# Two rows of results from four mixtures of rows, in two of three bands of two 3x3 convolutions

## The chip, the cores and the metric

The kernel runs on one core of a Trainium2 chip. Time is the device time in microseconds (us); lower is better. The core has a matrix engine (TensorE, PE in the profile, with its weight loads as PEld), two engines for elementwise work (VectorE, DVE; ScalarE, ACT), a general one (GpSimd, POOL) and a sequencer that issues transfers (SyncE, SP). TensorE writes its results to a small accumulator memory (PSUM)[...]; everything else works in SBUF, the on-chip memory.

## What is computed

The input x has the shape (4, 128, 64, 64): four images, 128 channels, 64 rows of 64. First comes an attention layer, then a block of two convolutions. Cut to what matters here:

```python
def conv_block(x, w1, alpha1, gamma1, beta1, w2, alpha2, gamma2, beta2):
    out = conv3x3(x, lsq_quantize(w1, alpha1))      # sum over 9 shifted views, pad 1
    out = relu(batchnorm(out, gamma1, beta1))       # mean and variance over all images and positions
    out = conv3x3(out, lsq_quantize(w2, alpha2))
    out = batchnorm(out, gamma2, beta2)
    return relu(out + x)

# layer 0: group norm, q, k, v, softmax(q k) v with 4 heads, projection, plus x
x = attention_block(x, ...)
x = conv_block(x, ...)
```

The quantised weights are whole numbers from -4 to 3 times alpha; the kernel keeps the whole numbers and moves alpha into the batch norm.

## The kernel before

Channels lie on the 128 partitions throughout. The attention takes the first 2230 us or so and isn't changed. It leaves its result y in DRAM (`y0[b]`), from which the convolutions load it.

**Bands.** Each image is cut into four bands of 16 rows (`BR = 16`), 16 bands in all (`bandlist`), numbered m = 0 to 15. A band tile holds 18 rows of 66 values: the 16 rows, one more above and below, and a zero column on each side (`border`, memsets on POOL). For accuracy, each band is split in two (`split`, L573 and L574): `hi` is the band copied into the type float32r (a CAST on VectorE), `lo` is the band minus `hi` (a TENSOR_TENSOR on VectorE). The band tile, `hi` and `lo` come from one pool of nine buffers (`kpool`).

**One convolution** (`layer`). A band gives 1024 results per channel, in two halves of 512, each in a PSUM bank. A half is 18 matmuls of 128x128 weights by 512 values: nine taps for `hi`, nine for `lo` (`conv`, L782), so a band has 36. The accumulators of a band are one two-bank tile of the pool `pss` (three tiles); the last band uses the two single banks of `psa`. For each band the program issues first the matmuls, then `prepare(m)`, which gets band m+2 ready, and then for each half the batch-norm statistics on VectorE (L848) and the copy of the accumulator to `cv[b]` on ScalarE (L849). Each engine works off its own instructions in this order; they wait for each other through semaphores, and the order is that written in the program.

**What prepare does.** In the first convolution (`first`) it issues on SP the load of band m+3 and splits band m+2. In band 2 it also loads the second layer's weights into `raw_w`, in band 6 it casts them into `wq[1]`, and in band 5 it runs `count_bad`, a check of the attention's sums with one tiny matmul. In the second convolution (`second`) it makes band m+2 from the first layer's results: `relu_rows` applies batch norm and relu with one ScalarE ACTIVATE (L891), then casts `hi` (L894) and subtracts for `lo` (L895), both on VectorE; band 0 is made specially in two pieces (L913, L916). It also loads y again for the residual (`load_res`).

**Between and after.** The first convolution's batch norm needs all its results, so TensorE runs only a few idle matmuls between the two. After the second, each piece of the result is scaled, added to y (L948), rectified (L949) and stored.

Of the kernel before, what the change touches and what calls it, by code (L numbers as in the profile page):

```python
# [16 lines left out]
F32 = mybir.dt.float32  # L17
AF = mybir.ActivationFunctionType
ALU = mybir.AluOpType
# [3 lines left out]
P = 128  # L23
# [3 lines left out]
TAPS = 9  # L27
FB = 512
# [6 lines left out]
F32R = mybir.dt.float32r  # L35
# [43 lines left out]
def _fast_body(ctx, tc, x, norm_w, norm_b, qkv_wt, qkv_b, proj_wt, proj_b,  # L79
               w1, alpha1, gamma1, beta1, w2, alpha2, gamma2, beta2, out, cnt):  # L80
    nc = tc.nc
    B, C, H, W = x.shape
# [3 lines left out]
    NB = N // FB  # L86
# [3 lines left out]
    PW = W + 2  # L90
# [48 lines left out]
    wq = [const.tile([P, TAPS, P], F32R, name="wq0")]  # L139
    wqd = dram.tile([P, TAPS, P], F32, name="wqd")  # L140
# [414 lines left out]
    def band_tile(name):  # L555
        return stack_tile(name).rearrange("p (r w) -> p r w", w=PW)

    def border(t, g):

        nc.gpsimd.memset(f32(t)[:, :, 0:1], 0.0)  # L560
        nc.gpsimd.memset(f32(t)[:, :, W + 1 : W + 2], 0.0)
        r0, r1 = g * BR - 1, g * BR + BR + 1
        if r0 < 0:
            nc.gpsimd.memset(f32(t)[:, 0, 1 : 1 + W], 0.0)
        if r1 > H:
            nc.gpsimd.memset(f32(t)[:, BR + 1, 1 : 1 + W], 0.0)
        lo, hi = max(r0, 0), min(r1, H)
        return f32(t)[:, lo - r0 : hi - r0, 1 : 1 + W], lo, hi

    def split(t, name):  # L570

        hi, lo = band_tile(f"hi{name}"), band_tile(f"lo{name}")
        nc.vector.tensor_copy(hi, f32(t))  # L573
        nc.vector.tensor_tensor(lo, f32(t), f32(hi), ALU.subtract)  # L574
        return hi, lo

    raw, ready = {}, {}

    def load_band(b, g):
        raw[b, g] = t = band_tile(f"t0_{b}_{g}")  # L580
        inner, lo, hi = border(t, g)
        nc.sync.dma_start(out=inner, in_=y0[b].rearrange("p (h w) -> p h w", w=W)[:, lo:hi, :])

    def split_band(b, g):
        ready[0, b, g] = split(raw[b, g], f"0_{b}_{g}")


    halves = [ppool.tile([P, HEADS, FB], F32, name=f"xh{i}", tag="p") for i in range(2)]
# [6 lines left out]
    st = small.tile([P, NB, 6], F32, name="st0", tag="st")  # L595
# [144 lines left out]
    todo, parts = [], {}  # L740
# [29 lines left out]

    bandlist = [(b, g) for b in range(B) for g in range(H // BR)]

    def conv(parts, ps, j, w):
        hi, lo = parts
        r0 = j * RB
        n = 0
        for part in (hi, lo):
            for tap in range(TAPS):  # L780
                kh, kw = divmod(tap, 3)
                nc.tensor.matmul(ps.rearrange("p (r w) -> p r w", w=W), w[:, tap, :],  # L782
                                 part[:, r0 + kh : r0 + kh + RB, kw : kw + W],
                                 start=(n == 0), stop=(n == 2 * TAPS - 1))
                n += 1

    def conv_tile(i, b, g):
        return pss.tile([P, 2, FB], F32, name=f"c{i}_{b}_{g}", tag="s")
# [16 lines left out]

    mid = ctx.enter_context(tc.tile_pool(name="mid", bufs=1))
    cv = [mid.tile([P, N], F32, name=f"cv{b}") for b in range(B)]
    raw_w = mid.tile([P, TAPS, P], F32, name="raw_w")
    wq.append(mid.tile([P, TAPS, P], F32R, name="wq1"))


    a_q, a_g, a_n = ([small.tile([P, 1], F32, name=f"{n}{i}") for i in range(2)]
# [21 lines left out]
    def layer(i, prepare, done):  # L834


        st = mid.tile([P, B * NB, 6], F32, name=f"st{i}")
        end = mid.tile([P, 15], F32, name=f"end{i}")
        nc.gpsimd.memset(end[:, 0:1], float((B * NB - 2) * FB))
        for m, (b, g) in enumerate(bandlist[:-1]):  # L840
            ps = done[m] if m < len(done) else conv_tile(i, b, g)
            for j in range(2):
                if m >= len(done):
                    conv(ready[i, b, g], ps[:, j, :], j, wq[i])
            prepare(m)
            for j in range(2):
                c = 2 * g + j
                nc.vector.bn_stats(st[:, b * NB + c, :], ps[:, j, :])  # L848
                nc.scalar.copy(cv[b][:, c * FB : (c + 1) * FB], ps[:, j, :])  # L849
        nc.vector.bn_aggr(end[:, 1:3], st.rearrange("p j s -> p (j s)")[:, : 6 * B * NB - 12])  # L850
        nc.vector.tensor_scalar(end[:, 2:3], end[:, 2:3], float((B * NB - 2) * FB), None, ALU.mult)
        b, g = bandlist[-1]
        for j in range(2):
            ps = psa.tile([P, FB], F32, name=f"c{i}_last{j}", tag="a")
            conv(ready[i, b, g], ps, j, wq[i])
            c = 2 * g + j
            nc.vector.bn_stats(end[:, 3 + 6 * j : 9 + 6 * j], ps)
            nc.scalar.copy(cv[b][:, c * FB : (c + 1) * FB], ps)
        prepare(len(bandlist) - 1)
        keep_warm(10)  # L860
        return batch_norm(i, end)
# [11 lines left out]
    def first(m):  # L873
        if m == 5:
            count_bad()
        if m == 2:
            nc.sync.dma_start(out=raw_w, in_=wqd)
        if m == 6:
            nc.vector.tensor_copy(wq[1], raw_w)
        if 0 < m < len(bandlist) - 3:  # L880
            load_band(*bandlist[m + 3])
        if m + 2 < len(bandlist) and m > 0:
            split_band(*bandlist[m + 2])

    a1, c1 = layer(0, first, early)

    def relu_rows(b, g, t, r0, r1):

        inner, lo, hi = t["inner"]
        a, e = max(r0 + g * BR - 1, lo), min(r1 + g * BR - 1, hi)  # L890
        nc.scalar.activation(inner[:, a - lo : e - lo, :],  # L891
                             cv[b].rearrange("p (h w) -> p h w", w=W)[:, a:e, :], AF.Relu,
                             bias=c1, scale=a1)
        nc.vector.tensor_copy(t["hi"][:, r0:r1, :], f32(t["t"])[:, r0:r1, :])  # L894
        nc.vector.tensor_tensor(t["lo"][:, r0:r1, :], f32(t["t"])[:, r0:r1, :],  # L895
                                f32(t["hi"])[:, r0:r1, :], ALU.subtract)

    def relu_band(b, g, pieces=((0, BR + 2),)):
        t = {n: band_tile(f"{n}1_{b}_{g}") for n in ("t", "hi", "lo")}
        t["inner"] = border(t["t"], g)  # L900
        for r0, r1 in pieces:
            relu_rows(b, g, t, r0, r1)
        ready[1, b, g] = t["hi"], t["lo"]


    b0, g0 = bandlist[0]
    t = {n: band_tile(f"{n}1_{b0}_{g0}") for n in ("t", "hi", "lo")}
    t["inner"] = border(t["t"], g0)
    hi_inner, lo_row, hi_row = border(t["hi"], g0)
    for r0, r1 in ((0, RB + 2), (RB + 2, BR + 2)):  # L910
        a, e = max(r0 + g0 * BR - 1, lo_row), min(r1 + g0 * BR - 1, hi_row)
        for dst in (hi_inner.bitcast(F32R), t["inner"][0]):
            nc.scalar.activation(dst[:, a - lo_row : e - lo_row, :],  # L913
                                 cv[b0].rearrange("p (h w) -> p h w", w=W)[:, a:e, :], AF.Relu,
                                 bias=c1, scale=a1)
# [26 lines left out]
    for b in range(B):  # L942
        for j in range(4):
            for p in range(2 if b == j == 0 else 1):
                n = HN // 2 if b == j == 0 else HN
                y = res[b, j][:, p * n : (p + 1) * n]
# [464 lines left out]
```

## Time and profile before

| what | us |
|---|---|
| median of three runs | 2547.48 (2546.02 to 2547.59) |
| the profiled execution, its own time | 2548.74 |
| the span of its profile | 2547.0 |
| first convolution's band 0 starts (TensorE) | 2233.99 |
| first convolution's last matmuls end, the idle ones start | 2375.12 |
| second convolution: first relu, first matmul | 2377.87, 2378.84 |
| second convolution's last matmul, end | 2516.46 |
| then batch norm, residual, relu and stores, to the end | 30.5 |

The matmul times are read from the trace in order of time; the last row is 2547.0 - 2516.46. In the 20 us from 2410 to 2430, in the middle of the second convolution, TensorE is busy all the time, VectorE for 8.25 us, ScalarE for 4.80 and POOL for 0.66, at the full granted clock. A busy TensorE means that matmuls follow each other without a pause, and the ends of matmuls are modelled. In the rows of the profile, a group is a line, an engine, an operation, output<-inputs with their sizes, the count, then busy time in us, the mean in ns, and the engine's idle time just before with what ended it.

### The profile page before, as it was taken

The page shows a single profiled execution, that of the slowest core. Times are in us where ns is not written, and L with a number is a line of the kernel's source. Part 1 is how long each engine was busy: PE and PEld are TensorE (multiplying, and loading weights), DVE is VectorE, ACT ScalarE, POOL GpSimd, SP SyncE. Part 2 cuts the span into 40 slices and gives each one's busy share as a digit, 9 for nine tenths or more (in the row PEclk, how much of TensorE's full clock was granted, in tenths as well). Part 3 has the DMA queues.
Part 4 walks back from the last instruction along what each step waited for, and adds up shares of the span by engine and source line. Part 5 has one row for each costly group of instructions (what it writes and reads, how often), then busy time and mean ns, then how long its engine had stood idle before and what let it go on. Part 6 is the DMA issues. An engine that isn't in the chain of part 4 may idle for free.

```text
span 2547.0 us, 65043 instructions
## 1 busy us (share of the span) xinstructions
PE 2509.0 (99%) x28708; PEld 1503.6 (59%) x28708; DVE 2137.2 (84%) x1402; ACT 2087.4 (82%) x2278; POOL 281.6 (11%) x461
## 2 busy tenths in 40 slices
PE   9999999999999999999999999999999999999995
PEld 6555555555555555555555555555555555577774
DVE  6899888889988889889988888889999999954445
ACT  5999888999988999999988899989999999911224
POOL 2111111111011111110111111111000011000000
PEclk9999999999999999999999999999999999999998
DMA  6877667788757667797766666796666666745004
GB/s 193 192 185 169 168 173 181 171 203 182 184 132 190 170 152 169 164 231 164 173 163 172 157 166 158 191 203 150 149 138 144 146 145 149 150 90 160 1 1 166
DMA packets 148954, 403.86 MB, mean 159 GB/s; under 512 B 59416, under 2 KB 60184, under 8 KB 120120
## 3 DMA queue, kind: packets, MB, share of 16 engines
q0 software_dynamic: 45840, 280.39, 48.2%
q1 hardware_dynamic: 100952, 113.60, 16.9%
q10 hardware_dynamic: 1872, 5.64, 0.6%
q8 instruction: 227, 3.72, 0.6%
q14 instruction: 63, 0.52, 0.1%
HBM read 107.48 MB, written 56.42 MB: 64 GB/s over the span
## 4 chain that ended last, share of the span: by engine, by line
PE 92%; issue 3%; DMA 2%; DVE 1%; ACT 1%; ACTq 0%; POOL 0%; SPq 0%; POOLq 0%; DVEq 0%
PE s L442 41%; PE acc L456 36%; PE c L782 9%; DMA rm<-p 2%; PE l L488 1%; PE pq L317 1%; PE pk L317 1%; PE po L317 1%; PE pv L317 1%; DVE r L471 1%; ACT p L444 0%; ACT res L949 0%; DMA xh<-in_x_dram 0%; PE c_last L782 0%; DVE res L948 0%
## 5 line engine op out<-in xcount | busy, mean ns | idle before, releaser
L444 ACT ACTIVATE p<-s 128x1024 f32<-128x1024 f32 x2048 | 1950.5, 1032 | 201.6 <-PE s L442 154.5
L471 DVE TENSOR_TENSOR r<-r,p 128x2048 f32<-128x2048 f32 x768 | 1758.2, 2289 | 65.0 <-ACT p L444 14.5
L442 PE MATMUL s<-q,k 64*128 64x512 f32 x8192 | 1138.6, 409 | 1.7 <-ACT p L444 0.9
L456 PE MATMUL acc<-p,v 128*32 128x256 f32 x16384 | 1026.4, 383 | 0.0
L442 PEld LDWEIGHTS s<-q,k 64*128 64x128 f32 x8192 | 715.4, 184 | 410.3 <-issue 165.3
L456 PEld LDWEIGHTS acc<-p,v 128*32 128x32 f32 x16384 | 462.4, 109 | 483.7 <-issue 248.5
L466 POOL DMA_DIRECT2D rm<-p x160 | 139.5, 872 | 800.4 <-ACT p L444 535.5
L849 ACT COPY cv<-c 128x512 f32<-128x512 f32 x60 | 35.2, 586 | 200.1 <-DVE st L848 200.1
L782 PE MATMUL c<-hi,wq 128*128 128x512 f32 x540 | 139.1, 401 | 1.3 <-issue 1.3
L782 PE MATMUL c<-lo,wq 128*128 128x512 f32 x540 | 138.5, 400 | 0.0
L848 DVE BATCH_NORM_STATS2 st<-c 128x6 f32<-128x512 f32 x60 | 41.9, 699 | 103.9 <-PE c L782 83.4
L782 PEld LDWEIGHTS c<-hi,wq 128*128 128x128 f32 x540 | 101.2, 188 | 30.3 <-issue 2.1
L782 PEld LDWEIGHTS c<-lo,wq 128*128 128x128 f32 x540 | 101.6, 188 | 27.2
L352 DVE SCALAR_TENSOR_TENSOR kst<-pk,b,kst 128x512 fp32r<-128x512 f32 x32 | 24.0, 751 | 83.6 <-PE s L442 68.5
L469 DVE TENSOR_TENSOR r<-p,p 128x2048 f32<-128x2048 f32 x32 | 73.2, 2288 | 12.1 <-ACT p L444 11.1
L352 DVE SCALAR_TENSOR_TENSOR qst<-pq,b,qst 128x512 fp32r<-128x512 f32 x32 | 24.0, 751 | 58.2 <-PE s L442 47.3
L356 POOL DMA_DIRECT2D qd<-qst x31 | 23.6, 760 | 262.7 <-DVE qst L352 220.8
L492 POOL DMA_DIRECT2D r<-rm x31 | 26.2, 844 | 220.4 <-DMA rm<-p 95.1
L356 POOL DMA_DIRECT2D kd<-kst x27 | 20.0, 740 | 175.8 <-DVE kst L352 167.2
L488 PE MATMUL l<-r,ones 128*32 128x256 f32 (+1 forms) x504 | 37.7, 382 | 0.0
L464 POOL DMA_DIRECT2D rm<-p x32 | 17.8, 557 | 176.8 <-ACT p L444 93.4
L351 ACT ACTIVATE kst<-pk,b 128x512 fp32r<-128x512 f32 x32 | 22.3, 699 | 18.2 <-PE pk L317 18.2
(149 smaller groups left out, 739.3 us busy)
## 6 DMA issues: line engine op xcount, KB each, us to landing
rm<-p POOLq DMA_DIRECT2D x192, 1024.0 KB, 7.9
q<-qd SPq DMA_DIRECT2D x248, 128.0 KB
r<-rm POOLq DMA_DIRECT2D x31, 1024.0 KB, 7.6
x<-in_x_dram SPq DMA_DIRECT2D x86, 256.0 KB
k<-kd SPq DMA_DIRECT2D x124, 128.0 KB
qd<-qst POOLq DMA_DIRECT2D x31, 512.0 KB, 5.3
kd<-kst POOLq DMA_DIRECT2D x27, 512.0 KB, 4.8
y<-x POOLq DMA_DIRECT2D x32, 256.0 KB, 6.2
```

The costliest lines, as they stand in the source:

```text
L317: nc.tensor.matmul(out[cs, :], w[:, cs], x, start=True, stop=True)
L352: nc.vector.scalar_tensor_tensor(lo, ps[what], bias, t[:, 0, :], ALU.add, ALU.subtract)
L356: (nc.sync if start else nc.gpsimd).dma_start(out=dst[b, j].rearrange("s p n -> p s n"), in_=t)
L442: nc.tensor.matmul(s[:, i, :], k[r, half, c0 : c0 + P], q[r, half, part, :], start=(part == 0), stop=(part == 1))
L444: nc.scalar.activation(pts[step][:, 2 * half : 2 * half + 2, :], s, AF.Exp, scale=SCALE)
L456: nc.tensor.matmul(acc[n][h * D : (h + 1) * D, cs], v[:, kt % KB, h * D : (h + 1) * D], pt[:, h, cs], start=(kt == 0 and half == 0), stop= ...
L466: nc.gpsimd.dma_start(out=msum[n], in_=pt, accum_op=ALU.add)
L469: nc.vector.tensor_tensor(rsum[n], pts[step - 1], pt, ALU.add)
L471: nc.vector.tensor_tensor(rsum[n], rsum[n], pt, ALU.add)
L488: nc.tensor.matmul(t["l"][h * D : (h + 1) * D, cs], ones, r[:, h, cs], start=first, stop=end)
L782: nc.tensor.matmul(ps.rearrange("p (r w) -> p r w", w=W), w[:, tap, :], part[:, r0 + kh : r0 + kh + RB, kw : kw + W], start=(n == 0), stop ...
L848: nc.vector.bn_stats(st[:, b * NB + c, :], ps[:, j, :])
```

## The change

In 8 bands of the first convolution (m = 3, 4, 6, 7, 9, 10, 12, 13) and 9 of the second (2, 3, 5, 6, 8, 9, 11, 12, 14), two neighbouring rows of results are computed together. Let d0 to d3 be the four input rows that two rows of results y0 and y1 need, and g0, g1, g2 the weights of the three rows of taps (each with its three columns). Then four mixtures of rows are made, d0 - d2, d1 + d2, d2 - d1 and d1 - d3, each is multiplied by its weights, g0, (g0+g2+g1)/2, (g0+g2-g1)/2 and g2, and with the four products c0, a0, a1, c1

y0 = c0 + a0 + a1,  y1 = a0 - a1 - c1.

Each product is a sum of three columns of taps, for an upper and a lower part: 6 matmuls of 8 rows x 64 = 512 values, and four products make 24 matmuls for the 16 rows of a band.

- `mixed` takes the place of `split` in these bands: `outer` holds the first and last mixtures in turn (one VectorE instruction on 1056 values), `inner` the two in the middle (two on 528). The upper parts are copies on ScalarE, the lower parts subtractions on VectorE. Of a mixed band's seven tiles four come from `kpool` (the band itself among them), three come from a new pool `upper` of six.
- `conv_by_two` issues the matmuls, the a products first. They need four banks: one `pss` tile for a, and for c in turn a second `pss` tile or the two `psa` banks.
- `rows_of_two` combines them in `cv[b]`: one ScalarE copy and four VectorE instructions of 512 values, in rows two apart. The statistics are then taken from `cv`, in SBUF, where they were taken from PSUM.
- `mix_weights` makes the two mixed sets of weights, four VectorE instructions for each convolution.
- In bands that stay plain, the upper part is a ScalarE copy, except in the first three bands of the first convolution and band 0 of the second.
- The second layer's weights lie in a `kpool` buffer in place of their own, and are loaded in band 5 instead of 2.

```diff
-    def split(t, name):
+    def split(t, name, beside=True):
         hi, lo = band_tile(f"hi{name}"), band_tile(f"lo{name}")
-        nc.vector.tensor_copy(hi, f32(t))
+        if beside:
+            nc.vector.tensor_copy(hi, f32(t))
+        else:
+            nc.scalar.copy(hi, f32(t))
         nc.vector.tensor_tensor(lo, f32(t), f32(hi), ALU.subtract)
         return hi, lo
...
+    BY_TWO = (set((3, 4, 6, 7, 9, 10, 12, 13)), set((2, 3, 5, 6, 8, 9, 11, 12, 14)))
+
+    def mixed(t, name):
+        t = f32(t)
+        outer, inner = (stack_tile(f"{n}{name}")[:, : BR * PW].rearrange("p (r w) -> p r w", w=PW)
+                        for n in ("vo", "vi"))
+        nc.vector.tensor_tensor(f32(outer), t[:, 0:BR, :], t[:, 2 : BR + 2, :], ALU.subtract)
+        odd, even = t[:, 1 : BR + 1 : 2, :], t[:, 2 : BR + 2 : 2, :]
+        nc.vector.tensor_tensor(f32(inner)[:, : BR // 2, :], odd, even, ALU.add)
+        nc.vector.tensor_tensor(f32(inner)[:, BR // 2 :, :], even, odd, ALU.subtract)
+        def part(n):
+            if n == "uo":
+                return stack_tile(f"{n}{name}")[:, : BR * PW].rearrange("p (r w) -> p r w", w=PW)
+            return upper.tile([P, BR, PW], F32R, name=f"{n}{name}", tag="u")
+        hi, lo = ([part(n + k) for k in "oi"] for n in "ul")
+        for u, v in zip(hi, (outer, inner)):
+            nc.scalar.copy(u, f32(v))
+        for u, v, w in zip(hi, (outer, inner), lo):
+            nc.vector.tensor_tensor(w, f32(v), f32(u), ALU.subtract)
+        return [(o[:, 0::2, :], i[:, : BR // 2, :], i[:, BR // 2 :, :], o[:, 1::2, :])
+                for o, i in (hi, lo)]
...
     def split_band(b, g):
-        ready[0, b, g] = split(raw[b, g], f"0_{b}_{g}")
+        m = bandlist.index((b, g))
+        way = mixed if m in BY_TWO[0] else lambda t, name: split(t, name, m < 3)
+        ready[0, b, g] = way(raw[b, g], f"0_{b}_{g}")
...
-    raw_w = mid.tile([P, TAPS, P], F32, name="raw_w")
     wq.append(mid.tile([P, TAPS, P], F32R, name="wq1"))
+    upper = ctx.enter_context(tc.tile_pool(name="upper", bufs=6))
+    wmix = mid.tile([P, 2, 3, P], F32R, name="wmix")
+
+    def mix_weights(i):
+        g0, g1, g2 = (f32(wq[i])[:, 3 * k : 3 * k + 3, :] for k in range(3))
+        h = f32(stack_tile(f"wsum{i}"))[:, : 3 * P].rearrange("p (t o) -> p t o", o=P)
+        nc.vector.tensor_tensor(h, g0, g2, ALU.add)
+        nc.vector.tensor_scalar(h, h, 0.5, None, ALU.mult)
+        for k, f in enumerate((0.5, -0.5)):
+            nc.vector.scalar_tensor_tensor(wmix[:, k, :, :], g1, f, h, ALU.mult, ALU.add)
+
+    def conv_by_two(parts, a, c, i):
+        for m, ps, w in ((1, a[0], wmix[:, 0, :, :]), (2, a[1], wmix[:, 1, :, :]),
+                         (0, c[0], wq[i][:, 0:3, :]), (3, c[1], wq[i][:, 6:9, :])):
+            n = 0
+            for part in parts:
+                for kw in range(3):
+                    nc.tensor.matmul(ps.rearrange("p (r w) -> p r w", w=W), w[:, kw, :],
+                                     part[m][:, :, kw : kw + W], start=(n == 0), stop=(n == 5))
+                    n += 1
+
+    def rows_of_two(a, c, y):
+        even, odd = (y.rearrange("p (r e w) -> p r e w", e=2, w=W)[:, :, e, :] for e in range(2))
+        a0, a1, c0, c1 = (u.rearrange("p (r w) -> p r w", w=W) for u in (*a, *c))
+        nc.scalar.copy(odd, a1)
+        nc.vector.tensor_tensor(even, odd, a0, ALU.add)
+        nc.vector.tensor_tensor(odd, a0, odd, ALU.subtract)
+        nc.vector.tensor_tensor(even, even, c0, ALU.add)
+        nc.vector.tensor_tensor(odd, odd, c1, ALU.subtract)
+
+    mix_weights(0)
...
         for m, (b, g) in enumerate(bandlist[:-1]):
+            if m in BY_TWO[i]:
+                a = conv_tile(i, b, g)
+                a = [a[:, j, :] for j in range(2)]
+                if sorted(BY_TWO[i]).index(m) % 2:
+                    c = [psa.tile([P, FB], F32, name=f"c{i}_{b}_{g}{j}", tag="a") for j in "xy"]
+                else:
+                    c = pss.tile([P, 2, FB], F32, name=f"c{i}_{b}_{g}z", tag="s")
+                    c = [c[:, j, :] for j in range(2)]
+                conv_by_two(ready[i, b, g], a, c, i)
+                prepare(m)
+                y = cv[b][:, 2 * g * FB : (2 * g + 2) * FB]
+                rows_of_two(a, c, y)
+                for j in range(2):
+                    nc.vector.bn_stats(st[:, b * NB + 2 * g + j, :], y[:, j * FB : (j + 1) * FB])
+                continue
...
-        if m == 2:
-            nc.sync.dma_start(out=raw_w, in_=wqd)
+        if m == 5:
+            raw["w"] = f32(stack_tile("raw_w"))[:, : TAPS * P].rearrange("p (t o) -> p t o", o=P)
+            nc.sync.dma_start(out=raw["w"], in_=wqd)
         if m == 6:
-            nc.vector.tensor_copy(wq[1], raw_w)
+            nc.vector.tensor_copy(wq[1], raw["w"])
+        if m == 14:
+            mix_weights(1)
...
-        nc.vector.tensor_copy(t["hi"][:, r0:r1, :], f32(t["t"])[:, r0:r1, :])
+        nc.scalar.copy(t["hi"][:, r0:r1, :], f32(t["t"])[:, r0:r1, :])
...
     def relu_band(b, g, pieces=((0, BR + 2),)):
+        if bandlist.index((b, g)) in BY_TWO[1]:
+            t = band_tile(f"t1_{b}_{g}")
+            inner, lo, hi = border(t, g)
+            nc.scalar.activation(inner, cv[b].rearrange("p (h w) -> p h w", w=W)[:, lo:hi, :],
+                                 AF.Relu, bias=c1, scale=a1)
+            ready[1, b, g] = mixed(t, f"1_{b}_{g}")
+            return
```

More of the change, by code (lines that the diff above doesn't have):

```diff
@@ L577, in _fast_body @@
     raw, ready = {}, {}
+    bandlist = [(b, g) for b in range(B) for g in range(H // BR)]
+    BY_TWO = (set((3, 4, 6, 7, 9, 10, 12, 13)), set((2, 3, 5, 6, 8, 9, 11, 12, 14)))
[18 more added lines that the diff above has]
+                for o, i in (hi, lo)]
     def load_band(b, g):
@@ L769, in _fast_body @@
         run_weights(3)
-    bandlist = [(b, g) for b in range(B) for g in range(H // BR)]
     def conv(parts, ps, j, w):
```

## The prediction

> **What bounds the kernel now.** I read the busy totals first, then the chain of work that ended last over the convolutions, then the same stretch in slices of 20 us, then the groups of VectorE and ScalarE by shape, and last the order of time inside one band. TensorE is busy nearly all the time:
>
> ```profile
> PE 2509.0 (99%) x28708; PEld 1503.6 (59%) x28708; DVE 2137.2 (84%) x1402; ACT 2087.4 (82%) x2278; POOL 281.6 (11%) x461
> ```
>
> The attention is not touched, so only the last 310 us matter. In the chain, the second convolution is one unbroken run of matmuls:
>
> ```profile
> 2378.84 129.02 PE c L782 x540
> 2507.86 8.60 PE c_last L782 x36
> ```
>
> 129.02 / 540 = 0.2389 us a matmul, so a band of 36 takes 8.60 us. The slices (columns: stretch, its length, busy time of PE, PEld, DVE, ACT, POOL, granted clock, DMA) show who has room:
>
> ```profile
> 2410.00:2430.00 20.00, 20.00 (x86) 15.78 (x85) 8.25 (x9) 4.80 (x6) 0.66 (x8) 1.00 0.00 1
> ```
>
> VectorE is free for 11.75 us of 20, ScalarE for 15. Prices, from the groups:
>
> ```profile
> L895 DVE TENSOR_TENSOR lo<-t,hi 128x1188 fp32r<-128x1188 f32 x15 | 20.9, 1397 | 0.5
> L371 DVE TENSOR_TENSOR v<-pv,bvn 128x512 f32<-128x512 f32 x8 | 5.5, 683 | 0.0
> L688 DVE BATCH_NORM_STATS2 st<-x 128x6 f32<-128x512 f32 x24 | 16.2, 685 | 0.0
> L916 DVE TENSOR_TENSOR lo<-t,hi 128x528 fp32r<-128x528 f32 x1 | 0.7, 707 | 0.5 <-ACT t L913 0.5
> L849 ACT COPY cv<-c 128x512 f32<-128x512 f32 x60 | 35.2, 586 | 200.1 <-DVE st L848 200.1
> L891 ACT ACTIVATE t<-cv,bc,ba 128x1152 f32<-128x1152 f32 x8 | 10.7, 1353 | 0.0
> ```
>
> Last, how a plain band hands over from VectorE to ScalarE and back (order of time, second convolution):
>
> ```profile
> 2413.45 0.70 DVE L848 BATCH_NORM_STATS2 st<-c 128x6 f32<-128x512 f32 x1 [2.36 <-PE c L782]
> 2414.19 0.59 ACT L849 COPY cv<-c 128x512 f32<-128x512 f32 x1 [5.40 <-DVE st L848]
> 2414.81 0.70 DVE L848 BATCH_NORM_STATS2 st<-c 128x6 f32<-128x512 f32 x1 [0.65 <-ACT cv L849]
> 2415.54 0.58 ACT L849 COPY cv<-c 128x512 f32<-128x512 f32 x1 [0.76 <-DVE st L848]
> 2416.02 1.36 ACT L891 ACTIVATE t<-cv,bc,ba 128x1152 f32<-128x1152 f32 x1
> 2417.48 0.78 DVE L894 CAST hi<-t 128x1188 fp32r<-128x1188 f32 x1 [1.97 <-ACT t L891]
> 2418.29 1.40 DVE L895 TENSOR_TENSOR lo<-t,hi 128x1188 fp32r<-128x1188 f32 x1
> ```
>
> Statistics and copies alternate, then ScalarE makes the relu of the band two ahead, and VectorE stands still 1.97 us for it. Today this is free: TensorE has the next band ready. Starts also show that independent instructions overlap by about 0.09 us (2418.29 to the next start is 1.31 for a duration of 1.40), while one that needs the previous result starts about 0.03 after its end.
>
> [...] Here the clock column was still 1.00 up to 2523.00 and 0.55 in the next microsecond, with the last matmul ending at 2518.7: over 4.3 us.
>
> **The change part by part.**
>
> *TensorE.* A mixed band has 24 matmuls instead of 36: 5.73 us, 2.87 less. There are 8 in the first convolution and 9 in the second: 17 x 2.87 = 48.7 us, if TensorE stayed the bound.
>
> *VectorE, preparing a mixed band.* Sum of 1056, two of 528, then two remainders of 1056. Issue distances 1.17 + 0.62 + 0.62 + 1.17 + 1.17 = 4.75 us. Each remainder needs a ScalarE copy of 1056. I take 1.17 us for it: [...] and 1.27, which the relu rows give (1.353 at 1152, 0.84 ns less per element); 1.03 is the floor, if it had only the fixed part of the 512 copy. The first copy starts at 1.3 and ends at 2.5, as the third sum does; the second ends at 3.75, the first remainder at 3.7. So about 0.25 us of waiting: 5.0 us. It is 4.8 at 1.03 and 5.1 at 1.27.
>
> *VectorE, finishing a mixed band.* One ScalarE copy of an accumulator (0.59, done while VectorE prepares), four sums of 512 with one operand in PSUM, three followed by a dependent one (0.72 each) and one by an independent one (0.60), then two statistics at 0.61: 2.76 + 1.22 = 4.0 us. Whether rows two apart cost extra isn't shown: 0 to 0.1 each; I take 0.
>
> *A plain band.* Before, statistics took 2.05 us with their wait, and split 2.1. Now the upper copy is ScalarE's (1.28 us at 1188 by the same slope as above). The order of the built kernel puts the plain band two ahead of a mixed one always right after the statistics of a plain band. So from the first statistics on: second copy starts at 2.08, next ScalarE instruction at 2.57; first convolution: upper copy ends 3.85, remainder at 3.95, plus 1.31: 5.3 us. Second: relu to 3.9, upper copy to 5.2, remainder at 5.3: 6.6 us. Of these 1.9 and 3.2 us VectorE only waits, with the sums for the next finished band queued behind the remainder. Nothing hides that wait any longer if VectorE is the bound.
>
> *Three bands, steady.* TensorE: 2 x 5.73 + 8.60 = 20.1 us, before 25.8. VectorE: 2 x (5.0 + 4.0) + 5.3 = 23.3 in the first convolution, + 6.6 = 24.6 in the second. So the bound moves to VectorE and its waits on ScalarE, and of 5.7 us a round only 2.5 and 1.2 are gained.
>
> *Small parts.* Mixed weights: one sum, one scaling, two fused ones of 384 (0.56, 0.36, 0.61, 0.61 by rows of these shapes): VectorE reaches the first statistics at 2259.9 instead of 2258.16. The second set (2.1) lies under TensorE's last two plain bands. The limit check costs VectorE about 1.0 us in band 5, since its matmul follows that band's, done by then. The load of the second weights moves from band 2 to 5 on SP's queue; its cast falls into the wait of a plain band. A band load lands about 4 us after its issue (moved between 2316.2 and 2319.1 for a memset at 2315.2) and is issued a band ahead on SP, whose buffer waits are for instructions VectorE has passed: cost 0, up to 4 us once if one came late. POOL's memsets take 0.13 us and go ahead likewise.
>
> *First convolution, summed.* From 2259.9 to the end of preparing band 13, VectorE's queue holds 8 preparations (40.0), 6 finishings (24.0), 3 plain rounds (15.9), two plain statistics without a split (4.1), the check (1.0): 85.0, so 2344.9. Band 13's accumulator is freed by band 11's copies 2.7 later: 2347.6. Then TensorE alone: 5.73 + 2 x 8.60, end 2370.5; before, conv ended at 2375.1. Gain 4.6.
>
> *Second, from the first relu (2377.87) as 0.* Preparing band 2 ends at 12.0. Statistics of band 0 and waiting for the relu of band 3: 4.0. Then up to the end of preparing band 12: 7 preparations (35.0), 6 finishings (24.0), 3 plain rounds (19.8): 94.8. Band 10's copies free the accumulator at 97.5; TensorE then runs bands 12 to 15, 5.73 + 8.60 + 5.73 + 8.60, to 126.2 (bands 13 to 15 are prepared by 101.4, 110.4, 115.7). Before: 2516.46 - 2377.87 = 138.6. Gain 12.4.
>
> Sum 17.0 us: span 2547.0 to 2530.0; the profiled run's 2548.74 is 1.3 above the median, so off the median 2547.48 the forecast is **2530.5 us**. A change under 0.2% (about 5 us) couldn't be told from none.
>
> **Rivals.**
>
> 1. *VectorE bound, but the plain bands' waits vanish* (ScalarE overlaps more than I think). 3.2 x 3 + 1.9 in the second and 1.9 x 3 in the first: 17 us more gain, 2513. Against it: the 1.97 us in the trace. Chance 0.08.
> 2. *TensorE stays the bound*: 2547.5 - 48.7 = 2499. It needs VectorE under 20.1 a round; even bare instruction distances are 2 x 8.75 + 2.7 = 20.2. Chance 0.03.
> 3. *Slower: the matmul clock.* TensorE now idles about 3 us in one place of a round in the first convolution and 4.5 in the second, before the second mixed band, whose accumulator waits for the plain band's statistics. The 4.3 us of the trace are that near. [...] A short relapse (f = 0.1) costs nothing, since finished accumulators lie over 5 us ahead of VectorE. Chance 0.17 for slower, in which I put a VectorE price over 10.3 us a mixed band too.
> 4. *No difference*: the same mechanism with about 1.1 us more per mixed band (10.1 instead of 9.0), say ScalarE copies of 1.7 us. Chance 0.10.
>
> My case has 0.62, its own range 2523 (copies at 1.03, -4 us, and some overlap) to 2540 (copies at 1.27, +2.5; strided sums at +0.1, +5). The range for 8 in 10 is 2512 to 2552. Faster: 0.62 + 0.08 + 0.03 = 0.73.
>
> **What would show it.** The chain should name VectorE and ScalarE lines in the convolutions rather than one run of matmuls; VectorE busy 8 to 9 tenths there, TensorE about 8; its matmuls still 0.239 apart. The remainder of plain bands should wait near 1.9 and 3.2 us on the upper copy. The preparing of a mixed band should span 5.0, the finishing 4.0. Wrong would be a clock below 1.00 inside a convolution, or ScalarE copies of 1056 outside 1.0 to 1.3 us.

## The result, and the profile after it

The changed kernel takes **2527.24 us** (median of 6 runs, 2525.50 to 2530.38) against 2547.53 us for the kernel before in the same session: a ratio of 0.9923, with a 95% interval of 0.9910 to 0.9936. The forecast was 2530.5. The profiled execution took 2527.63 us, with a span of 2526.1.

The trace divides it like this. The first convolution is measured here from its first matmul to the second's first relu, the second from that relu to the start of the last statistics.

| stage, us | before | after | gain |
|---|---|---|---|
| first matmul of the first convolution, at | 2233.99 | 2231.79 | 2.2 |
| first convolution, to the first relu | 143.88 | 140.05 | 3.8 |
| second convolution, to the last statistics | 138.61 | 123.48 | 15.1 |
| from there to the end of the span | 30.5 | 30.8 | -0.3 |

The sum is the 20.9 us between the two spans. Nothing was edited in the first row's stage, and the experiments come back to it. Below, a round is three bands in a row, two mixed and one plain, and the tail of a convolution is what comes after the last full round, from TensorE's start into its last bands on. First the totals (busy time of each engine, its share of the span, instructions):

```profile
PE 2472.3 (98%) x28504; PEld 1472.2 (58%) x28504; DVE 2217.1 (88%) x1518; ACT 2124.9 (84%) x2306; POOL 281.3 (11%) x461
```

They say little, being averages over a kernel that is nearly all attention. TensorE lost 36.7 us of work and the time fell by 20. The chain that ended last tells why. Where the kernel before had one piece of 129 us of matmuls, the second convolution is now (start, us, engine, tile and line):

```profile
2414.95 1.23 DVE li L607
2416.19 0.62 DVE st L928
2416.83 0.59 ACT cv L929
2417.45 0.71 DVE st L928
2418.18 0.58 ACT cv L929
2418.76 1.21 ACT t L974
...
2420.05 1.20 ACT hi L977
2421.27 1.40 DVE lo L978
...
2472.39 8.58 PE c L814 x36
...
2486.70 8.60 PE c_last L814 x36
```

VectorE (DVE) sets the time, and around a plain band it hands over to ScalarE (ACT) and back, one behind the other. TensorE is in the chain only from 2466 on, for its last four bands: nothing that VectorE still prepares holds it up there. Two slices of the second convolution (columns as before: stretch, length, PE, PEld, DVE, ACT, POOL, granted clock, DMA):

```profile
2410.00:2430.00 20.00, 17.25 (x73) 13.27 (x72) 16.12 (x21) 9.54 (x11) 0.42 (x5) 1.00 0.01 2
2435.00:2455.00 20.00, 16.57 (x60) 12.71 (x59) 16.11 (x20) 10.80 (x12) 0.42 (x5) 0.83 0.00 0
```

VectorE went from 8.25 us of 20 to 16.1, TensorE from 20 to 17. The second row has a granted clock of 0.83: TensorE had half its clock for part of it (0.50 granted for 6.83 us from 2441.35 on). VectorE's missing 3.9 us are found in the order of time, at the place that the prediction showed for the kernel before:

```profile
2416.10 0.69 DVE L928 BATCH_NORM_STATS2 st<-c 128x6 f32<-128x512 f32 x1
2417.45 0.70 DVE L928 BATCH_NORM_STATS2 st<-c 128x6 f32<-128x512 f32 x1 [0.65 <-ACT cv L929]
2421.27 1.40 DVE L978 TENSOR_TENSOR lo<-t,hi 128x1188 fp32r<-128x1188 f32 x1 [3.12 <-ACT hi L977]
```

After the second statistics VectorE stands still for 3.12 us, while ScalarE makes the copy, the relu and the upper part. The waits of VectorE over both convolutions (who, for whom, us in total, times, longest):

```profile
DVE lo L978 <- ACT hi L977: 14.4, 5, 3.2
...
DVE lo L577 <- ACT hi L576: 6.3, 4, 1.7
...
DVE cnt L951 <- PE nbad L950: 2.3, 1, 2.3
```

The last line is VectorE's wait for the count of the limit check (`count_bad`). The rows of the new operations, grouped by shape (busy us, mean ns):

```profile
L607 DVE TENSOR_TENSOR li<-vi,ui 128x1056 fp32r<-128x1056 f32 x17 | 21.4, 1259 | 0.0
...
L605 ACT CAST uo<-vo 128x1056 fp32r<-128x1056 f32 x17 | 18.3, 1077 | 75.3 <-DVE vo L594 69.3 <-issue 6.0
...
L870 DVE TENSOR_TENSOR cv<-c,cv 128x512 f32<-128x512 f32 x17 | 11.8, 691 | 0.6
```

The lower part lasts 1.259 us, where a straight line through two VectorE rows of before (0.683 at 512 and 1.397 at 1188) gives 1.258. The sums in rows two apart last 0.69, as contiguous ones did before (0.683). The ScalarE copy of 1056 lasts 1.077, less than the 1.17 that the prediction took.

### The profile page after: what moved, and what is told of

Read it like the earlier page. It is cut to its first block, busy times and chain, and to the rows that moved or that the text cites. A ratio compares the mean times of both kernels' runs of the same rounds, so it can differ in the third digit from the quotient of the medians.

```text
span 2526.1 us, 64792 instructions
## 1 busy us (share of the span) xinstructions
PE 2472.3 (98%) x28504; PEld 1472.2 (58%) x28504; DVE 2217.1 (88%) x1518; ACT 2124.9 (84%) x2306; POOL 281.3 (11%) x461
## 3 DMA queue, kind: packets, MB, share of 16 engines
q0 software_dynamic: 45840, 280.39, 48.7%
## 5 line engine op out<-in xcount | busy, mean ns | idle before, releaser
L466 POOL DMA_DIRECT2D rm<-p x160 | 139.2, 870 | 799.0 <-ACT p L444 574.0
L469 DVE TENSOR_TENSOR r<-p,p 128x2048 f32<-128x2048 f32 x32 | 73.2, 2288 | 10.7 <-ACT p L444 9.7
L605 ACT CAST uo<-vo 128x1056 fp32r<-128x1056 f32 x17 | 18.3, 1077 | 75.3 <-DVE vo L594 69.3
L929 ACT COPY cv<-c 128x512 f32<-128x512 f32 x26 | 15.2, 586 | 61.2 <-DVE st L928 61.2
L814 PE MATMUL c<-hi,wq 128*128 128x512 f32 x234 | 60.4, 402 | 1.3 <-ACT hi L1003 1.3
L814 PE MATMUL c<-lo,wq 128*128 128x512 f32 x234 | 60.1, 401 | 0.0
L860 PE MATMUL c<-ui,wmix 128*128 128x512 f32 x102 | 35.4, 461 | 17.7 <-ACT cv L929 14.7
L814 PEld LDWEIGHTS c<-hi,wq 128*128 128x128 f32 x234 | 43.7, 188 | 14.9 <-issue 2.1
L814 PEld LDWEIGHTS c<-lo,wq 128*128 128x128 f32 x234 | 44.0, 188 | 11.8
```

The source lines that it names most:

```text
L466: nc.gpsimd.dma_start(out=msum[n], in_=pt, accum_op=ALU.add)
L469: nc.vector.tensor_tensor(rsum[n], pts[step - 1], pt, ALU.add)
```

## The experiments

The theory was the prediction's likeliest case, made sharper by the trace: **VectorE's own queue, with its waits for ScalarE, sets each round of three bands; TensorE has slack.** The main rival was that TensorE still sets it, through the number of its matmuls or through its clock. This table holds all kernels run. The convolutions are those of one profiled execution each. A ratio is that to the kernel before, run beside it.

| kernel | median us | ratio, 95% interval | first conv. | second conv. |
|---|---|---|---|---|
| before | 2547.53 | 1 | 143.88 | 138.61 |
| changed | 2527.24 | 0.9923 [0.9910, 0.9936] | 140.05 | 123.48 |
| changed, again | 2528.07 | 0.9928 [0.9916, 0.9939] | 137.43 | 123.45 |
| upper parts on VectorE | 2523.48 | 0.9902 [0.9886, 0.9919] | 134.36 | 124.40 |
| fewer matmuls | 2531.25 | 0.9936 [0.9919, 0.9952] | 139.29 | 126.02 |
| one more on VectorE | 2538.06 | 0.9961 [0.9947, 0.9976] | 142.39 | 129.30 |
| finish first | 2520.90 | 0.9892 [0.9876, 0.9909] | 136.88 | 117.48 |
| finish first, again | 2520.06 | 0.9890 [0.9876, 0.9904] | 136.48 | 117.46 |
| idle time filled | 2530.05 | 0.9924 [0.9908, 0.9941] | 138.28 | 127.20 |
| finish first, upper parts of the first on VectorE | 2523.05 | 0.9894 [0.9877, 0.9910] | 140.09 | 117.45 |
| finish first, late count | 2518.81 | 0.9878 [0.9862, 0.9895] | 135.00 | 117.57 |
| finish first, late count, again | 2517.79 | 0.9881 [0.9867, 0.9896] | 134.87 | 117.58 |
| second convolution only | 2532.82 | 0.9936 [0.9919, 0.9952] | 143.80 | 123.52 |
| best of each | 2516.09 | 0.9878 [0.9862, 0.9895] | 133.72 | 117.54 |

Where a kernel was profiled twice, the second convolution repeats to 0.1 us; the changed kernel's first one differs by 2.6 us, for a reason given below. So the column of the first convolution is read together with the length of its rounds.

### Does TensorE's work still count? Fewer matmuls

Three plain bands of each convolution leave out the lower part's products, 108 matmuls in all; the results are accordingly less exact.

```diff
-        for part in (hi, lo):
+        for part in (hi,) if half else (hi, lo):
...
-                    conv(ready[i, b, g], ps[:, j, :], j, wq[i])
+                    conv(ready[i, b, g], ps[:, j, :], j, wq[i], m in ((5, 8, 11), (4, 7, 10))[i])
```

> The changed kernel, but the plain bands 5, 8, 11 of the first convolution and 4, 7, 10 of the second leave out the products of their lower part: 6 x 18 = 108 matmuls less, and the result is less accurate. Theory (VectorE bound in the middle of both convolutions): no faster than 2 us, and those 2 from the limit check in band 5, which waits for that band's matmuls. Rival (TensorE still bound, or bound through its halved clock): 108 x 0.239 = 26 us faster, some 2501.

108 matmuls are 25.8 us of TensorE, and the time did not fall: 2531.25 us, 4 us above the changed kernel. So TensorE's work does not set the rounds. VectorE's second statistics of a plain band come every 23.7 us in both traces (2393.70, 2417.45, 2441.19 in the changed kernel; 2393.69, 2417.41, 2441.14 here). The loss lies behind the last round. TensorE's orders of time, in this kernel

```profile
2466.29 1.65 PE L860 MATMUL c<-ui,wmix 128*128 128x512 f32 x3 [5.17 <-ACT cv L929]
2467.74 1.48 PE L860 MATMUL c<-li,wmix 128*128 128x512 f32 x3
```

and in the changed one:

```profile
2466.37 1.00 PE L860 MATMUL c<-ui,wmix 128*128 128x512 f32 x3 [1.01 <-ACT cv L929]
2467.21 0.87 PE L860 MATMUL c<-li,wmix 128*128 128x512 f32 x3
```

Both start at the same time, but after a pause of 5.17 us three matmuls take 1.28 us from start to start (2467.74 to 2469.02 for the next group) instead of 0.72; the granted clock is 0.54 from 2465 to 2470. From here on TensorE alone sets the end, and its last four groups of nine start at 2489.05 rather than 2486.54: these 2.5 us are the second convolution's whole loss (126.02 against 123.48).

### Does VectorE's work count? One more on VectorE

The first statistics of each mixed band are taken twice.

```diff
-                for j in range(2):
+                for j in (0, 0, 1):
```

> The changed kernel with the first statistics instruction of each mixed band done twice on VectorE (0.61 us each). Theory: 12 of the 17 lie on the path (6 in each convolution, the rest under TensorE's last bands), so 12 x 0.61 = 7.3 us slower, or about 6 where two of them go into the wait of the limit check: 2533 to 2535. Rival (TensorE bound): no difference.

10.8 us slower by the medians. In the trace a third statistics instruction adds 0.72 us from start to start (2405.69 to 2407.62 for three, 2401.47 to 2402.67 for two), so 17 of them are 12.2. A round has two: it went from 23.74 to 25.2 us in the second convolution and from 22.37 to 23.81 in the first, about 1.44 each, which is twice 0.72. Within a round VectorE's time counts in full. The theory's 7.3 us took 0.61 us for what costs 0.72; its 12 instructions make 8.6. The two convolutions of this trace are 2.3 and 5.8 us longer than in the changed kernel's first execution. In the first, about 2 us came back at the count, whose wait fell from 2.3 to 0.3; in the second, 1.5 us are a half-clock stretch in the tail (2474.93 to 2479.40 for four groups of three matmuls, at a granted clock of 0.66 from 2475 to 2480; 2466.37 to 2469.34 in the changed kernel, at 1.00). Of the rest of the 10.8, 1.9 us lie ahead of the convolutions in these two executions (first matmul at 2233.68 and 2231.79).

### Is the wait for ScalarE lost time? Finish first, and the copies back

`finish first` moves no work between engines. In mixed bands whose band m+2 is plain, `prepare(m)` stands behind the finishing of band m instead of ahead of it, so VectorE has 3.8 us of finishing to do while ScalarE makes the relu and the upper part.

```diff
-                prepare(m)
+                finish_first = m + 2 < len(bandlist) and m + 2 not in BY_TWO[i]
+                if not finish_first:
+                    prepare(m)
...
+                if finish_first:
+                    prepare(m)
```

> The changed kernel, but where a mixed band m has a plain band m+2, the mixed band is finished first and the plain one prepared after it, so that ScalarE can make relu and upper part while VectorE adds rows. Theory: the waits of 3.1 us (second convolution) and 1.75 us (first) in front of the remainder of a plain band fall to about 1.2 us, for the copy of an accumulator behind the copies of the plain band: 3 x 1.9 + 3 x 0.55, some 7 us faster than the changed kernel, 2520. Rival (the waits are hidden anyway, or the later preparation starves TensorE): no difference, or slower.

> Mixed bands finished before the next plain band is prepared, on the same chip as the changed kernel: 6 to 7 us less than it, most of it in the second convolution, 117.5 us; the rival, that the two earlier results differed by the chip, gives under 3 us.

2520.90 and 2520.06 us. Run beside the changed kernel (2528.07) it is 8.0 us less, somewhat more than the 6 to 7 expected, and the intervals do not touch. The rival, a difference between chips, falls. The second convolution went from 123.5 to 117.5, its round from 23.74 to 21.77. The waits of VectorE in this kernel:

```profile
DVE cv L869 <- ACT cv L868: 10.3, 9, 1.1
...
DVE lo L982 <- ACT hi L981: 1.8, 1, 1.8
```

The 14.4 and 6.3 us for the upper parts are gone but for one of 1.8 at the start. In their place VectorE waits 1.14 us nine times for the accumulator's copy, now behind the statistics' own copies on ScalarE: of 20.7 us of waiting 8.6 were saved, the rest changed place.

`upper parts on VectorE` undoes the ScalarE copies of plain bands alone.

```diff
-        way = mixed if m in BY_TWO[0] else lambda t, name: split(t, name, m < 3)
+        way = mixed if m in BY_TWO[0] else lambda t, name: split(t, name)
...
-        nc.scalar.copy(t["hi"][:, r0:r1, :], f32(t["t"])[:, r0:r1, :])
+        nc.vector.tensor_copy(t["hi"][:, r0:r1, :], f32(t["t"])[:, r0:r1, :])
```

> The changed kernel with the upper parts of all plain bands back on VectorE. Theory (VectorE and its waits on ScalarE set the time, and the copy on ScalarE lies on that path): in the first convolution a plain round falls from 5.1 us to about 4.0 (statistics 2.0, cast 0.70, remainder 1.31), in the second from 6.5 to about 6.0, because the wait for the relu stays and the copy behind it goes; with the start of the second convolution about 4 us faster than the changed kernel, some 2523. Rival (moving the copies off VectorE is part of the gain): VectorE gets 10 casts of 0.70 back, up to 7 us slower, some 2534.

2523.48 us: by the medians this part of the change was a loss of 3.8 us. The intervals of the ratios overlap, so the reading rests on the rounds. A VectorE copy takes 0.76 us (1188 values) and replaces a wait of 1.74 in the first convolution, whose last round falls from 22.36 to 21.34. In the second the relu is waited for all the same (1.92 us before the copy), and the round falls only from 23.74 to 23.34; a half-clock stretch in the tail (granted clock 0.50 from 2460 to 2465) gave that back (124.40 against 123.48).

Both remedies together in the first convolution:

> The order of the kernel that finishes mixed bands first, and the upper parts of the first convolution's plain bands on VectorE. Theory (a wait that the order already fills cannot be saved twice): VectorE gets five copies of 0.76 us = 3.8 us more and saves no wait, so it is 3 to 4 us slower than finishing first alone: 2524. Rival (ScalarE's copy costs by something else than the wait of VectorE, so moving it back gains as it did alone, 3.8 us): 2517.

2523.05 us. The ratio is that of finishing first alone, and the four runs spread over 4.3 us, so the times decide nothing here; the trace does. The first convolution is 3.2 us longer than with finishing first alone. Its two full rounds last 23.26 and 22.58 us instead of 22.44 and 21.77, each 0.8 longer by one copy of 0.76: the copies cost their own time where no wait is left to save. 1.4 of the 3.2 us are not the copies': TensorE's first four groups of three matmuls in the tail take 4.36 us (from 2347.70) instead of 2.95 (from 2345.30), with a granted clock of 0.75 from 2345 to 2350. A wait is saved once.

### What does the clock cost? Idle time filled, and the late count

In the first mixed band of each round TensorE gets 12 further matmuls, into an accumulator that the real ones then start anew.

```diff
+                if not sorted(BY_TWO[i]).index(m) % 2:
+                    for k in range(12):
+                        nc.tensor.matmul(a[1].rearrange("p (r w) -> p r w", w=W), wmix[:, 1, k % 3, :],
+                                         ready[i, b, g][0][2][:, :, k % 3 : k % 3 + W],
+                                         start=True, stop=True)
                 conv_by_two(ready[i, b, g], a, c, i)
```

> In the first of the two mixed bands of each round TensorE gets 12 more 512-column matmuls, written into an accumulator before its real ones start it anew, so the results do not change. That is 12 x 0.239 = 2.87 us a round and 9 x 2.87 = 25.8 us in all, put where TensorE idles 3 us a round and its clock was seen to halve. Theory (VectorE sets the round, TensorE's slack is free): the gaps shrink to under 1 us, the granted clock of both convolutions is 1.00 throughout, and the time is that of the changed kernel or up to 4 us less (the limit check's wait of 2.3 us falls to about 1): 2523 to 2528. Rival (TensorE's matmuls are still what the rounds last): up to 25.8 us slower, 2553.

2530.05 us: by the medians 2.8 above the changed kernel, by the ratios to the kernel before the same, where the added matmuls are 25.8. So the rival falls, but the theory's range is passed too. In the second convolution TensorE is now full, at the full clock (a slice of its columns as above):

```profile
2430.00:2450.00 20.00, 20.00 (x85) 15.78 (x84) 16.07 (x22) 8.86 (x10) 0.48 (x6) 1.00 0.00 1
```

It has 468 real matmuls and 60 more there, 528 x 0.2389 = 126.1 us, plus 1 us to the first: 127.1, and it lasted 127.20. There had been 123.48 - 112.8 = 10.7 us of room for the 14.3 us added. The full clock bought nothing in that convolution. In the first the wait for the count fell to 0.3 us, as the theory had it, and the convolution lasted 138.28 us with 11.5 us more of matmuls; that lies between the changed kernel's two executions (140.05 and 137.43), so a gain from the full clock is not shown by this run. (The slices from 2260 to 2270 still had clocks of 0.67 and 0.65: the first pause stands ahead of the first added matmuls.)

`second convolution only` has the first convolution as before (no mixed bands, no first mixed weights, upper parts on VectorE).

```diff
-    BY_TWO = (set((3, 4, 6, 7, 9, 10, 12, 13)), set((2, 3, 5, 6, 8, 9, 11, 12, 14)))
+    BY_TWO = (set(), set((2, 3, 5, 6, 8, 9, 11, 12, 14)))
...
-    mix_weights(0)
```

> The first convolution as before the change, the second as changed (its plain upper parts on ScalarE too). Theory (the two convolutions gain independently): the first lasts 141.1 us again, the second 123.5, so the time is 3.8 us above the changed kernel: 2531; three quarters or more of the gain are the second's. Rival (the first convolution gains nothing of its own, the mixed weights and the count eat it): 2527.

2532.82 us. The first convolution lasts 143.80 (before 143.88; the expectation's 141.1 counts to the last matmul), the second 123.52 (changed 123.48): the two gains simply add. The second had its half-clock stretch here too (0.77 granted from 2445 to 2450, 0.55 from there to 2455), after a pause of 3.44 us at 2448.72, with no effect on its length.

`late count` reads the limit check's count in band 6 instead of band 5; the edit is shown against `finish first`.

```diff
-        nc.vector.tensor_copy(cnt, nbad[0:1, 0:1])
+        return nbad
...
         if m == 6:
+            nc.vector.tensor_copy(cnt, raw["nbad"][0:1, 0:1])
```

> The order that finishes mixed bands first, and VectorE reads the limit check's count one band later, when TensorE has long written it. Theory (VectorE is the bound there, so its wait for the count, 1.6 us with this order and 2.3 us in the changed kernel, is lost time): 1.5 us faster than finishing first alone, 2519.4. Rival (the wait is refilled by a later one): 2520.9.

> The same with the count read one band later: theory, 1.5 us less than finishing first alone (the wait of 1.6 us goes and nothing takes its place); rival, within 0.5 us of it.

2518.81 and 2517.79 us, 2.1 and 2.3 less than without it, and the first convolution is 1.6 to 1.9 us shorter. The intervals of the ratios overlap. The runs side by side do not (2517.45 to 2518.28 against 2519.22 to 2521.59).

### The changed kernel once more

> The changed kernel itself once more, beside the two reordered ones on the same chip. The two convolutions last as before (first 140.0 us from its first matmul to the first relu, second 123.5 us). The part ahead of the convolutions was 2.2 us shorter in its one profile than in that of the kernel before, with no edit there: theory (that is one execution against another) it is anywhere from 2231.5 to 2236 us here; rival (the change shortens it) it ends at 2232 again. Time 2527 to 2529.

2528.07 us (2524.38 to 2536.20). Its convolutions begin at 2231.07, below the range that the theory gave; this run alone would leave the rival standing. But over all 14 traces of this case that moment lies between 2230.5 and 2236.1 with no edit to the code ahead of it, and the kernel before, at 2233.99, is in the middle: 2233.99 against 2231.79 is one execution against another. The second convolution lasts 123.45 again, the first 137.43 instead of 140.05, and two places account for that. VectorE's read of the count, in the first execution

```profile
2292.23 0.14 DVE L951 CAST cnt<-nbad 1x1 int32<-1x1 f32 x1 [2.31 <-PE nbad L950]
```

and in the second:

```profile
2290.47 0.15 DVE L951 CAST cnt<-nbad 1x1 int32<-1x1 f32 x1 [0.99 <-PE nbad L950]
```

and TensorE's start into its last bands, in the first

```profile
2344.62 0.98 PE L860 MATMUL c<-ui,wmix 128*128 128x512 f32 x3 [2.00 <-ACT cv L929]
2345.44 1.20 PE L860 MATMUL c<-li,wmix 128*128 128x512 f32 x3
2346.44 1.48 PE L860 MATMUL c<-ui,wmix 128*128 128x512 f32 x3
```

and in the second:

```profile
2342.85 0.98 PE L860 MATMUL c<-ui,wmix 128*128 128x512 f32 x3 [0.49 <-ACT cv L929]
2343.68 0.88 PE L860 MATMUL c<-li,wmix 128*128 128x512 f32 x3
2344.39 0.87 PE L860 MATMUL c<-ui,wmix 128*128 128x512 f32 x3
```

Four groups of three matmuls take 4.38 us to the next in the first execution (2344.62 to 2349.00) and 2.97 in the second. The count's wait differs by 1.32 us, these bands by 1.41: together 2.7, where the whole convolution differs by 2.6. Both are the clock. Ahead of the count, band 4's matmuls start at 2274.74 in the first execution and at 2274.29 in the second, and the granted clock is 0.50 for 6.83 us in the first and for about 3.4 in the second (0.91 from 2270 to 2275, 0.75 from there to 2280); from there to the count's own matmul are 17.26 and 15.95 us. From 2345 to 2350 it is 0.66 in the first and 1.00 in the second. A stretch in the middle of the second execution (0.69 from 2320 to 2325, 0.97 from there to 2330, so about 3.4 us at half clock) cost nothing: its round lasts 22.37 us, as in the first. So the clock does cost time, but only where TensorE is waited for: at the count and in the tails.

### The best of each

The first convolution with its plain upper parts on VectorE and the old order, the second with finishing first, and the late count. The edit is shown against `finish first, late count`.

```diff
-                finish_first = m + 2 < len(bandlist) and m + 2 not in BY_TWO[i]
+                finish_first = i == 1 and m + 2 < len(bandlist) and m + 2 not in BY_TWO[i]
...
-        way = mixed if m in BY_TWO[0] else lambda t, name: split(t, name, m < 3)
+        way = mixed if m in BY_TWO[0] else lambda t, name: split(t, name)
```

> The first convolution with its plain upper parts on VectorE and the old order, the second with mixed bands finished first, and the count read one band later. Theory (each convolution keeps the round it had alone: 21.3 us in the first, against 21.8 with finishing first, and 21.8 in the second): first convolution 133.5 us from its first matmul to the first relu, second 117.5, about 1.3 us less than finishing first with the late count: 2516.5. Rival (TensorE's round of 20.1 us is so near that its clock's relapses take the gain back): the first convolution lasts 135 us or more.

2516.09 us (2515.51 to 2516.73), the fastest of all: 31 us under the kernel before and 11 under the changed one. Each convolution kept what it had alone, 133.72 and 117.54. That it beats finishing first with the late count rests on the trace of the first convolution (1.2 us) and on the medians, from runs on different chips; the ratios' intervals are the same.

## Why the prediction came out as it did

**That the bound moves to VectorE was right.** The chain names VectorE and ScalarE; taking 25.8 us from TensorE gained nothing, and 1.44 us more for VectorE lengthened each round by 1.44. Of TensorE's 48.7 us, as said, most were not to be had. The rival in which TensorE stays the bound fell with the same runs; so did that of no difference, which needed 10.1 us a mixed band, where it takes 8.64.

**Preparing a mixed band** was put at 5.0 us and takes 4.80 (2402.67 to 2407.47). The mis-sized term is ScalarE's copy, taken as 1.17 us, the author's estimate below the 1.27 that the slope of the relu rows gave (0.867 at 576, 1.353 at 1152); it lasts 1.077, and no wait is left inside the preparation. **Finishing** was put at 4.0 us and takes 3.84: two of the four sums, not three, are followed only after 0.72 us, the other two after 0.6. Rows two apart cost nothing.

**A plain band** was put at 5.3 and 6.6 us and takes 5.09 and 6.48, of which VectorE waits 1.74 and 3.12 (1.9 and 3.2 said). The first figure is 2272.02 to 2277.11 in the trace, the second 2416.10 to 2422.58. The upper copy was taken as 1.28 and lasts 1.19. The mechanism, a remainder that holds up the finishing queued behind it, is what finishing first undid, for 6 to 8 us. That the waits vanish by themselves (the rival at 2513) was wrong.

**The rounds** were put at 23.3 and 24.6 us and take 22.37 and 23.74. The difference in the second, 0.86, is 2 x 0.2 + 2 x 0.16 + 0.12 = 0.84. Over the eight preparations, six finishings and three plain rounds of the prediction's sum this makes 8 x 0.2 + 6 x 0.16 + 3 x 0.12 = 2.9 us, and the second convolution gained 2.7 more than forecast (15.1 against 12.4).

**The first convolution's gain** was put at 4.6 us and is 3.8. That the two lie so close is luck, since larger errors cancel. The smaller durations gave 8 x 0.2 + 6 x 0.16 + 3 x 0.2 = 3.2 us back here as well, and three things took them. First, the step "The limit check costs VectorE about 1.0 us in band 5, since its matmul follows that band's, done by then" failed: the check took 2.7 us (2289.58 to 2292.31), since band 5's matmuls were not done. TensorE had fallen to half clock twice before (0.50 granted for 3.41 and 6.83 us), after pauses of 3.03 and 3.24 us. Second, the half-clock stretch after 2344.62 cost 1.4 us in the tail. Third, VectorE reached the first statistics 26.6 us after the first matmul, not 25.9, with 1.3 us of waiting for a transfer before the mixed weights (2258.43 - 2231.79 against 2259.9 - 2233.99). These are 1.7 + 1.4 + 0.7 = 3.8 us. The transfers costed at nothing held otherwise: no other wait of VectorE in the convolutions names one.

**The matmul clock.** "Wrong would be a clock below 1.00 inside a convolution": it was below, in both. What failed is the step that set 4.3 us as the pause from which the clock falls. That number came from a slice of 1 us behind the kernel's last matmul and was only an upper bound: after pauses of 3.03 us, and once even of 1.73, the granted clock was 0.50. What held is the other step, that a short relapse costs nothing while finished accumulators lie ahead of VectorE: in the second convolution about 13 of the 84 matmuls of one round ran at half clock (from 2442.56 to 2448.18, 0.427 us each, which is 0.19 more than 0.239), a share f of 0.16, and the round grew by less than 0.1 us: TensorE's own round is then, as an estimate from these figures, 84 x 0.239 + 13 x 0.19 = 22.5 us, under the 23.74 that VectorE took. In the round with the count about 22 did, f = 0.26; the same estimate gives 24.3, over the first convolution's 22.37, and there VectorE did wait. So the slower rival had its mechanism right, but such a share came in one round of this trace only.

**The sum.** In the spans, 2526.1 against a forecast of 2530.0: the attention's 2.2 us of one execution and 2.7 from the second convolution, less 0.8 in the first and 0.3 behind the convolutions. The repeated run, with 6.4 + 15.2 in the convolutions, shows that the first convolution's gain was 3.8 us in one execution and 6.4 in another, by where the half-clock stretches fell. The median, 3.3 us under the forecast, contains that.

## What to carry to other kernels

When a change takes work from the busiest engine, price the round of the next one by start-to-start distances and add every wait that its queue will meet; then look which queued work could stand in front of the waiting instruction, since reordering gave more here (6 to 8 us) than moving the copy to the freer engine, which lost. A copy moved to another engine to unload the bound costs the bound the whole hand-over (1.74 and 3.12 us of waiting here), unless it has something else to do meanwhile. And TensorE with slack came back from some pauses, here of 1.73 us and more, at half clock: harmless in the middle of these rounds, but paid for in the tails and where a small result of TensorE's was read at once.

## What the runs showed of the hardware that was not expected

- TensorE's clock halved after shorter pauses than assumed, and the length of the pause alone does not decide it. In the changed kernel's trace the granted clock is 0.50 in five stretches inside the convolutions: for 3.41 us from 2263.86, 6.83 from 2274.10, 3.41 from 2301.40, 3.41 from 2345.78 and 6.83 from 2441.35. The pauses at their beginnings are of 3.03, 3.24, 1.73, 2.00 and 3.43 us. A pause of 2.75 us (to 2418.82) cost no clock: 1.00 from 2413 to 2425. The changed kernel's two executions have a pause of 1.73 us in the same place, up to 2299.89 and up to 2298.13. In the first the clock falls behind it (window, length, PE, PEld, DVE, ACT, POOL, granted clock, DMA share, GB/s):

```profile
2297.99:2301.40 3.41, 1.68 (x7) 1.24 (x7) 1.80 (x3) 2.65 (x4) 0.00 (x0) 1.00 0.62 131
2301.40:2304.82 3.42, 3.42 (x9) 2.66 (x8) 3.38 (x5) 0.01 (x1) 0.24 (x3) 0.50 0.36 83
```

In the second it stays:

```profile
2295.00:2300.00 5.00, 3.27 (x14) 2.27 (x13) 3.22 (x5) 2.74 (x4) 0.00 (x0) 1.00 0.67 132
2300.00:2305.00 5.00, 5.00 (x23) 3.93 (x22) 4.93 (x8) 0.00 (x0) 0.24 (x3) 1.00 0.56 115
```

What decides it besides the length of the pause is not shown.
- The first convolution of two executions of one kernel differed by 2.6 us, at two places that are both half-clock stretches (1.32 and 1.41 us), while the rounds that VectorE sets repeat to 0.1 us (22.35 to 22.37 in the first convolution of both, 23.74 to 23.81 in the second).
- VectorE instructions of 512 values in rows two apart, one operand in PSUM, last as long as contiguous ones did (0.691 us against 0.683).
